# A two-layer graph network: the second pair of tiles prepared by the scheme of the later pairs

## The chip, the cores and the metric

The kernel runs on one core of a Trainium2 chip. The metric is the device time of one execution in microseconds (us); the time of a kernel is the median of its runs. Next to it stands one execution taken by the hardware profiler; all traces shown here are of such executions.

## What is computed

128 graphs of 64 nodes with 768 features (8192 rows) and one 0/1 adjacency matrix per graph go through two layers. Cut to what matters:

```python
# layer 0:  h = relu(layernorm(x));  deg, rdeg = row sums of adj and of its transpose, 0 replaced by 1
ctx = adj @ (h @ Wadj.T + badj) / deg  +  adj.T @ (h @ Wrev.T + brev) / rdeg  +  h @ Wself.T + bself
rel = einsum('bij,bijr->bir', adj, E[rels]) @ Wr.T + br * deg  +  (the same, turned: E[rr], Wrr, brr)
x = x + ctx + rel                      # rels is the adjacency matrix itself
# layer 1:  h = relu(layernorm(x))
#   attention over each graph's neighbours, six heads of 128; elu, and a sigmoid gate of h @ H_w.T
x = x + gate * elu(attention) + (1 - gate) * h
```

## The kernel before, in words

The 8192 rows are 64 tiles of 128 rows (two graphs each), taken in 32 pairs. Pass 1 computes layer 0 for one pair after the other, pass 2 layer 1. The change is in pass 1 alone.

For each pair the layer 0 product has a left operand of two rows of blocks (the two tiles) by three blocks of features, times three by three blocks of weights. Each block `a00` to `a12` of the left operand has three parts side by side: h gathered over the neighbours and divided by the row degree, the same for the turned adjacency, and the tile's own h. From the second pair on the 18 block products are done as 15, by a scheme in which sums of operand blocks (`f1`, `f7`, ..., formed on VectorE by `form`) meet sums of weight blocks (`g1`, ..., formed once by `weights_sums`). The relation part is a product of counts (how often each value stands in a row of the adjacency matrix, 81 columns) with a small table `tabs` of 16-bit numbers.

`main(p)` (line 792) gives the product steps of a pair: one matmul of 128x256 a step, six to a block product. Pair 0 has 108 of them, 18 for each fill of a PSUM bank, and two last count products; the other pairs have 90 and one. A bank of pair 0 takes a count product just before VectorE's `add` reads it (from the third fill on), so steps 53, 71, 89 and 107 are followed by one. The banks are `pwa`, `pwb` and the two halves of `pwcd`.

The order of the work is written out by hand, for every engine and for the queue of SyncE (SP), which issues nearly all transfers. `merged` (line 259) runs a pair's steps and calls each entry of a list just before the product step whose number it bears. For pair 0 that list is `first` (line 969), which prepares pair 1; for pair p it is `beside(p)` (line 1011), with the numbers of `BESIDE` (line 86), which prepares pair p+1 and finishes pair p-1. Each engine works its part of the program in this order; an instruction that waits holds all behind it on its engine.

A pair in `SHARED` (line 778) is prepared in another way than the others. Before the change that is every pair from 2 on. The two ways differ in these steps:

- Statistics for the norm: `dev` (line 931) calls `moments` on ScalarE for a pair in `SHARED`, and `deviation` (line 313) on VectorE for the others; the power is on GpSimd in both (lines 332 to 334, or line 321).
- Own part: the others multiply h by an identity along with the neighbours (`operands`, line 738, with n = 3 parts, so 192 columns, line 754). A pair in `SHARED` has n = 2 (128 columns). Its own part is written a second time by ScalarE in a mixed order (`relu_mixed`, line 549), turned in 32x32 blocks by VectorE (`turn_own`, line 558, one buffer `hpt` for all tiles), stored to DRAM (`put_own`, line 563) and loaded back into the third part of the six blocks (`load_own`, line 574) in runs of 32 floats.
- Operand sets: the others make them two blocks at a time (`operand`, line 775) in a PSUM tile `pb`. A pair in `SHARED` makes all six in one batch (`operands_in_one`, line 769); its last two blocks use the bank pair `pwcd`. ScalarE copies the sets out (line 764).
- Degrees: the others by a matmul with a block of ones (`degrees`, line 649) and a reciprocal on VectorE. A pair in `SHARED` reduces on VectorE, inverts, turns (`turn_degrees`, line 600), and spreads them through DRAM (`put_degrees`, `get_degrees`); `over_row_degrees` (line 622) makes the scaled adjacency.
- Counts: `spread_counts` (line 703) lays them out in `c3s`; the others turn them on TensorE (`count_t`, line 728) and copy them on ScalarE. A pair in `SHARED` turns them in blocks on VectorE (`turn_counts`) and goes through DRAM (`put_counts`, `get_counts`).

The table `tabs` is made of three parts in `table_part` (line 526): ScalarE rounds a part to 16 bits, VectorE takes the rest for the next, and SP stores it in its places (line 538). The count products of pair 0 are the first to read it.

Of the kernel before, what the change touches and what calls it, by code (L numbers as in the profile page):

```python
# [156 lines left out]
def kernel(  # L157
# [45 lines left out]
    nc = tc.nc  # L203
# [10 lines left out]
    NP = NT // 2  # L214
# [188 lines left out]
    with ExitStack() as px:  # L403
# [154 lines left out]
        def turn_own(t):  # L558

            h = HPT[t] = work.tile([P, D], F32, name="hpt", bufs=1)  # L560
            nc.vector.transpose(h, HP[t])

        def put_own(t):
            nc.sync.dma_start(H0D[t].rearrange("(b p) n -> p b n", p=P),
                              HPT[t].rearrange("p (b n) -> p b n", b=KB))
# [8 lines left out]
        def load_own(p, *names):  # L574

            for n in names:
                k, q = int(n[1]), int(n[2])
                nc.sync.dma_start(
                    new_operand(p, n)[:, 2].rearrange("p b (a n) -> p (b a) n", a=NQ),
                    H0D[2 * p + k].rearrange("(b i) (f n) -> (i f) b n", i=Q, n=Q)[  # L580
                        :, q * KQ * NQ : (q + 1) * KQ * NQ, :])
# [18 lines left out]
        def turn_degrees(p):  # L600


            row_degrees(p)
            d = dgs
            v = d[:, :4].rearrange("p (k d) -> p k d", k=2)
            nc.vector.tensor_scalar(v, DGR[p], 1.0, None, op0=OP.max)
            nc.vector.reciprocal(v, v)
            RD[p] = small.tile([P, Q], F32, name="dt", bufs=1)
            nc.vector.transpose(RD[p], d)

        def put_degrees(p):
            nc.sync.dma_start(RDD[p].rearrange("c (b n) -> b c n", n=Q), RD[p])

        def get_degrees(p):
            rd = RD[p] = work.tile([P, 4, N], F32, name="rd", bufs=1)
            for g in range(GT):
                at = RDD[p][0:4, g * N : (g + 1) * N]
                nc.sync.dma_start(rd[g * N : (g + 1) * N],
                                  bass.AP(tensor=at.tensor, offset=at.offset,
                                          ap=[[0, N], *at.ap]))  # L620

        def over_row_degrees(p):
            rd = RD[p].rearrange("p (k d) n -> p k d n", k=2)
            for d in range(2):
                nc.vector.tensor_mul(rts[p % 2][:, :, d, :], ADF[p][:, :, 1 - d, :], rd[:, :, d, :])

        def prep_c(p):


            af, ab = ADF[p], AB[p]  # L630
            cnt = CNT[p] = work.tile([P, 2, NROW], BF16, name="cnt", bufs=1)
            if p not in SHARED:
                row_degrees(p)
            dg = DGR[p]
            nc.vector.tensor_scalar(cnt[:, :, NCNT : NCNT + 2], dg, 1.0, None, op0=OP.min)
            nc.vector.memset(cnt[:, :, NCNT + 2 : NCNT + 3], 1.0)
            gr = GR[p] = work.tile([P, 2, 2, N], BF16, name="gr")
            wo = WO[p] = work.tile([P, 2, 2, N], BF16, name="wo")
            ov = work.tile([P, 2, 2, N], BF16, name="ov", bufs=1)
            nc.vector.tensor_scalar(ov, ab, float(NG), None, op0=OP.is_gt)  # L640
            nc.vector.tensor_scalar(wo, ov, float(DIGIT - 1), 1.0, op0=OP.mult, op1=OP.add)
            nc.vector.scalar_tensor_tensor(gr, ov, -float(NG), ab, op0=OP.mult, op1=OP.add)
            nc.vector.tensor_scalar(ov, ab, float(2 * NG), None, op0=OP.is_gt)
            nc.vector.scalar_tensor_tensor(wo, ov, float(DIGIT * DIGIT - DIGIT), wo,
                                           op0=OP.mult, op1=OP.add)
            nc.vector.scalar_tensor_tensor(gr, ov, -float(NG), gr, op0=OP.mult, op1=OP.add)
            SUM[p] = work.tile([P, 2, 2, NG], F32, name="sum")
# [38 lines left out]
        def count(p, k):  # L686
            ids_worth(p, k)
            ids_sum(p, k)
# [14 lines left out]
        def spread_counts(p):  # L703
            for f, n, at, v0, w in ((0, 3, 0, 0, Q), (3, 1, 0, Q, Q), (4, 2, 0, Q, Q), (6, 2, 0, 2 * Q, R2),
                                    (6, 1, R2, 2 * Q, Q - R2), (7, 1, R2, 3 * Q - R2, 2 * R2 - Q)):
                c3 = c3s.rearrange("p k i (f n) -> p k i f n" if p in SHARED else
                                   "p k i (n f) -> p k i f n", f=NQ)
                put = nc.gpsimd.tensor_copy if p in SHARED else nc.scalar.copy
                put(c3[:, :, f // NQ, f % NQ : f % NQ + n, at : at + w],
                    CNT[p][:, :, None, v0 : v0 + w].to_broadcast([P, 2, n, w]))  # L710

        def turn_counts(p):
            ct = CT_T[p] = work.tile([P, 4, P], BF16, name="ct", tag="eq", bufs=1)
            nc.vector.transpose(ct.rearrange("p a n -> p (a n)"),
                                c3s.rearrange("p k i n -> p (k i n)"))

        def put_counts(p):
            nc.sync.dma_start(CTD[p].rearrange("(q p) n -> p q n", p=P), CT_T[p])

        def get_counts(p):  # L720
            ct = work.tile([P, 2, 2, P], BF16, name="cntT", bufs=2)
            nc.sync.dma_start(
                ct.rearrange("p k i n -> p (k i n)").rearrange("p (b n) -> p b n", n=Q),
                CTD[p].rearrange("(b i) (f n) -> (i f) b n", i=Q, n=Q))
            for k in range(2):
                CT_T[p, k] = ct[:, k]

        def count_t(p, k):
            pn = pss.tile([P, 2, 512], F32, name="pb")[:, 0, :P].bitcast(BF16).rearrange(
                "p (i n) -> p i n", i=2)  # L730
            if k == 0:
                CT_T[p] = work.tile([P, 2, 2, P], BF16, name="cntT", bufs=2)
            cn = CT_T[p, k] = CT_T[p][:, k]
            for i in range(2):
                nc.tensor.transpose(pn[:, i, :], c3s[:, k, i, :], identb)
            nc.scalar.copy(cn, pn)

        def operands(p, *calls, last=False):


            n = 2 if p in SHARED else 3
            if last:
# [32 lines left out]
        def operand(p, *calls):  # L775
            operands_out(p, operands(p, *calls), *calls)

        SHARED = range(2, NP)

        def form(p, *names):  # L780

            for n in names:
                s0, x, s1, y = A_SUMS[n]
                if n in IN_PLACE:
                    OPS[p, n] = OPS[p, IN_PLACE[n]]
                else:
                    new_operand(p, n)
                signed(OPS[p, n], s0, OPS[p, x], s1, OPS[p, y])
# [155 lines left out]
        def norm(p, k):  # L944
            t = 2 * p + k
            if p not in SHARED:
                scaled_mean(*DEV[t])
            for f in (relu_mixed, relu) if p in SHARED else (relu,):
                f(t, DEV[t][0])
# [8 lines left out]
        def degrees_and_norms(p):  # L958
            deg(p)
            for k in range(2):  # L960
                norm(p, k)
            one_over(DEG[p])
            over_degrees(p, DEG[p])

        def weights_sums(*names):
            for n in names:
                sum_of_weights(bw, n)
# [14 lines left out]
            (23, lambda: prep(1)),  # L982
            (24, lambda: devs(1)),
            (26, lambda: table_part(2)),
            (34, lambda: degrees_and_norms(1)),
            (30, lambda: weights_sums("w", "v")),
            (36, lambda: weights_sums("g6")),
            (38, lambda: weights_sums("u", "g14")),
            (38, lambda: count_t(0, 0)),
            (40, lambda: prep_c(1)),  # L990
            (44, lambda: count(1, 0)),
            (45, lambda: count_t(0, 1)),
            (52, lambda: count(1, 1)),
            (54, lambda: operand(1, (1, 2))),
            (54, lambda: operand(1, (1, 1))),
            (58, lambda: digits(1)),
            (60, lambda: load(2)),
            (60, lambda: weights_sums("g12", "g5")),
            (64, lambda: operand(1, (0, 0))),
            (64, lambda: operand(1, (0, 2))),  # L1000
            (66, lambda: weights_sums("g8")),
            (73, lambda: form(1, "f1", "f7", "f4")),
            (76, lambda: weights_sums("g11", "g3")),
            (80, lambda: operand(1, (1, 0))),
            (80, lambda: operand(1, (0, 1))),
            (84, lambda: spread_counts(1)),
            (84, lambda: count_t(1, 0)),
            (91, lambda: form(1, "f8", "f9", "f2")),
            (92, lambda: count_t(1, 1))]

        def beside(p):

# [572 lines left out]
```

## Time and profile before

| | before |
|---|---|
| runs | 2323.54 to 2324.08 us |
| median of 3 runs | 2323.63 us |
| the profiled execution's own time | 2323.5 us |
| span of its trace (first to last instruction) | 2321.7 us |
| mean granted TensorE clock | 0.997 |

An engine's row in a timeline has the start in us from the span's start, the length, the engine, the line of the code and the instruction with what it writes and reads; "xN" are N instructions in a row, merged. In square brackets stands how long the engine was idle before, and what ended that. PE is TensorE's matmuls, PEld its weight loads, DVE is VectorE, ACT ScalarE, POOL GpSimd, and SPq the issue of transfers by SyncE. A product step of 32-bit numbers is two MATMUL records.

### The profile page before, as it was taken

How to read it: one execution, taken by the hardware profiler on the slowest of the kernel's cores; microseconds unless marked ns; L12 is line 12 of the kernel's file. 1: busy time of each engine (PE TensorE's matmuls, PEld its weight loads, DVE VectorE, ACT ScalarE, POOL GpSimd, SP SyncE). 2: the span in 40 equal slices, each digit the busy share in tenths (PEclk: the TensorE clock that was granted, in tenths of full speed). 3: DMA queues.
4: the chain of work that ended last, by engine and by line, in shares of the span. 5: the costliest groups of instructions: out<-in, count | busy, mean ns of one | idle time of the engine just before them, and what ended most of it. 6: DMA issues, size and time to landing. Idle time of an engine off the chain costs nothing.

```text
span 2321.7 us, 35387 instructions
## 1 busy us (share of the span) xinstructions
PE 2295.5 (99%) x11321; PEld 1638.6 (71%) x11321; DVE 1935.2 (83%) x3741; ACT 1319.2 (57%) x4083; POOL 309.4 (13%) x739
## 2 busy tenths in 40 slices
PE   9999999999999999999999999999999999999996
PEld 7888888888888888888888885444444444444444
DVE  8877777777777777777777777899999999999998
ACT  3454454454454444543543523777777777777776
POOL 1111111111111111111111111000001100000011
PEclk9999999999999999999999999999999999999998
DMA  5445545545546546546546555567666677667766
GB/s 191 92 100 130 136 101 135 130 101 136 129 101 146 118 103 147 116 108 148 110 107 151 109 140 165 138 159 166 157 163 159 158 173 168 158 157 168 168 158 144
DMA packets 831048, 321.68 MB, mean 139 GB/s; under 512 B 633236, under 2 KB 781063, under 8 KB 830860
## 3 DMA queue, kind: packets, MB, share of 16 engines
q1 hardware_dynamic: 821788, 294.99, 52.9%
q0 software_dynamic: 8928, 24.38, 5.9%
q8 instruction: 89, 1.46, 0.3%
q14 instruction: 99, 0.81, 0.1%
q10 hardware_dynamic: 144, 0.04, 0.0%
HBM read 151.90 MB, written 141.85 MB: 127 GB/s over the span
## 4 chain that ended last, share of the span: by engine, by line
PE 96%; DVE 2%; DMA 1%; issue 0%; SPq 0%; ACT 0%; DVEq 0%; ACTq 0%
PE pwa L826 21%; PE pwb L826 18%; PE pwcd L826 15%; PE pma L1143 14%; PE pmb L1143 12%; PE pmd L1143 5%; PE pmc L1143 5%; PE pb L754 3%; PE ps L1343 1%; PE pwcd L810 1%; PE pwcd L754 1%; DMA weights<-in_wadj_t_dram 1%; DVE f L1380 0%; PE pmc L1343 0%; PE pwa L810 0%
## 5 line engine op out<-in xcount | busy, mean ns | idle before, releaser
L826 PE MATMUL pwa<-weights,op 128*128 128x256 f32 x2304 | 529.6, 379 | 0.3 <-DVE x L818 0.3
L826 PEld LDWEIGHTS pwa<-weights,op 128*128 128x128 f32 x2304 | 427.5, 190 | 56.0 <-issue 1.1
L826 PE MATMUL pwb<-weights,op 128*128 128x256 f32 x1932 | 451.4, 381 | 0.0
L826 PEld LDWEIGHTS pwb<-weights,op 128*128 128x128 f32 x1932 | 361.9, 190 | 51.4 <-issue 0.8
L355 DVE TENSOR_TENSOR op<-op 128x768 f32<-128x768 f32 x310 | 290.2, 945 | 94.6 <-ACT op L764 91.7
L826 PE MATMUL pwcd<-weights,op 128*128 128x256 f32 x1560 | 357.8, 379 | 0.0
L826 PEld LDWEIGHTS pwcd<-weights,op 128*128 128x128 f32 x1560 | 296.1, 190 | 40.1
L1143 PE MATMUL pma<-weights,op_f 128*128 128x512 f32 x620 | 297.0, 593 | 0.1
L1196 ACT ACTIVATE pr<-pr 128x128 f32<-128x128 f32 x768 | 226.2, 297 | 68.5 <-DVE pr L1185 68.4
L764 ACT COPY op<-pb 128x512 f32<-128x512 f32 (+1 forms) x132 | 70.8, 618 | 331.9 <-PE pb L754 331.8
L1143 PEld LDWEIGHTS pma<-weights,op_f 128*128 128x128 f32 x620 | 117.5, 190 | 147.7 <-issue 125.4
L1143 PE MATMUL pmb<-weights,op_f 128*128 128x512 f32 x372 | 175.1, 592 | 0.0
L553 ACT ACTIVATE hp<-x,rn 128x768 f32<-128x768 f32 x60 | 109.3, 1821 | 108.3 <-POOL rn L334 108.3
L1196 ACT ACTIVATION_READ_ACCUMULATOR pr<-pr 128x1 f32 x768 | 145.0, 189 | 0.0
L326 ACT ACTIVATE hf<-x 128x768 f32<-128x768 f32 x64 | 53.6, 838 | 160.3 <-DVE x L862 148.7
L332 POOL TENSOR_SCALAR rn<-su 128x1 f32<-128x1 f32 x124 | 25.8, 208 | 844.8 <-ACT hf L327 527.9
L1143 PEld LDWEIGHTS pmb<-weights,op_f 128*128 128x128 f32 x372 | 70.7, 190 | 89.0 <-issue 87.3
L1143 PE MATMUL pmc<-weights,op_f 128*128 128x512 f32 x248 | 121.6, 592 | 0.0
L1303 ACT ACTIVATE pb<-a,mx 128x64 f32<-128x64 f32 x360 | 119.6, 335 | 2.2 <-DVE mx L1294 2.1
L818 DVE TENSOR_TENSOR x<-pwcd,x 128x256 f32<-128x256 f32 x127 | 53.3, 420 | 80.2 <-PE pwcd L810 80.0
L684 DVE TENSOR_REDUCE sum<-eq 128x26 f32<-128x1664 bf16 x64 | 120.0, 1876 | 0.1
L1143 PE MATMUL pmb<-weights,h 128*128 128x512 f32 x248 | 119.8, 604 | 0.0
(248 smaller groups left out, 3904.4 us busy)
## 6 DMA issues: line engine op xcount, KB each, us to landing
x<-in_x_dram SPq DMA_DIRECT2D x64, 384.0 KB
h<-ht SPq DMA_DIRECT2D x256, 96.0 KB
out_dram<-x SPq DMA_DIRECT2D x64, 384.0 KB
hh<-hh SPq DMA_DIRECT2D x64, 384.0 KB
h<-h SPq DMA_DIRECT2D x64, 384.0 KB
x<-hh SPq DMA_DIRECT2D x64, 384.0 KB
out_dram<-f POOLq DMA_DIRECT2D x62, 384.0 KB, 7.6
h<-hpt SPq DMA_DIRECT2D x60, 384.0 KB
```

The costliest lines, as they stand in the source:

```text
L326: nc.scalar.activation(by, src, AF.Copy, scale=-1.0 / D, accum_out=sums[:, 0:1])
L332: nc.gpsimd.tensor_scalar(to[:, 0:1], sums[:, 1:2], 1.0 / D, EPS, op0=OP.mult, op1=OP.add)
L355: return (nc.vector.tensor_add if s1 == "+" else nc.vector.tensor_sub)(to, x, y)
L553: nc.scalar.activation(hp.rearrange("p (b f i) -> p b f i", b=KB, f=NQ), X[t].rearrange("p (b i f) -> p b f i", b=KB, f=NQ), AF.Relu, scal ...
L684: nc.vector.tensor_reduce(SUM[p][:, k], EQ[p, k], AX.X, OP.add)
L754: nc.tensor.matmul(to[:, g, :, i, :], H0[2 * p + k][o, kb * P : (kb + 1) * P], rts[p % 2][o, k, :n].rearrange("p s n -> p (s n)"), start=T ...
L764: nc.scalar.copy(a[:, :n].rearrange("p s h (g n) -> p g (s h) n", g=GT), ps[:, :, c * n * KQ * N : (c + 1) * n * KQ * N].rearrange("p g (x ...
L818: nc.vector.tensor_add(v, bank[b][:, :CQ], v)
L826: nc.tensor.matmul(bank[b][:, :CQ], OPS[p, an][:, s, q, :], bw[bn][:, (s * KQ + q) * CQ : (s * KQ + q + 1) * CQ], start=(first and q == s ...
L1143: nc.tensor.matmul(bank[p, b], operand(p, an)[:, q, :], bw2[bn][:, 2 * q * CQ : 2 * (q + 1) * CQ], start=(first and q == 0), stop=(q == KQ ...
L1196: nc.scalar.activation(PR[t][:, j, h, :], PR[t][:, j, h, :], AF.Copy, accum_out=to)
L1303: nc.scalar.activation(PB[t][:, h, :], AL[t][:, h, :], AF.Exp, bias=MX[t][:, h : h + 1], accum_out=DN[t][:, h : h + 1])
```

## The change

Pair 1 joins the pairs in `SHARED`. The list `first` is rewritten for that. `degrees_and_norms(1)`, three `operand` calls and two `count_t` calls of pair 1 leave it. In their place come `turn_degrees`, `put_degrees`, `get_degrees`, two norms, two turns of the own part with their stores, `over_row_degrees`, `load_own` for all six blocks, the counts' turn with its store and load, and one `operands_in_one`. `count_t(0, 1)` moves from step 45 to 39, `spread_counts(1)` from 84 to 66, and `g11` and `g3` get places of their own. `load(2)` keeps its number 60 and stands behind `load_own` in SP's queue. Of the forms only `f1` and `f7` are left in the list; `f4`, `f8`, `f9` and `f2` are made in `beside(1)`, since line 1016 asks for `SHARED`. `dev(1, k)` uses `moments` for the same reason. In `spread_counts` pair 1 still uses ScalarE, with the layout of `SHARED`.

```diff
-                put = nc.gpsimd.tensor_copy if p in SHARED else nc.scalar.copy
+                put = nc.gpsimd.tensor_copy if p > 1 else nc.scalar.copy
...
-        SHARED = range(2, NP)
+        SHARED = range(1, NP)
...
             (23, lambda: prep(1)),
             (24, lambda: devs(1)),
             (26, lambda: table_part(2)),
-            (34, lambda: degrees_and_norms(1)),
+            (27, lambda: turn_degrees(1)),
+            (28, lambda: put_degrees(1)),
             (30, lambda: weights_sums("w", "v")),
             (36, lambda: weights_sums("g6")),
+            (38, lambda: get_degrees(1)),
             (38, lambda: weights_sums("u", "g14")),
             (38, lambda: count_t(0, 0)),
+            (39, lambda: count_t(0, 1)),
+            (40, lambda: norm(1, 0)),
+            (40, lambda: norm(1, 1)),
             (40, lambda: prep_c(1)),
+            (43, lambda: turn_own(2)),
+            (44, lambda: put_own(2)),
             (44, lambda: count(1, 0)),
-            (45, lambda: count_t(0, 1)),
+            (47, lambda: turn_own(3)),
+            (48, lambda: put_own(3)),
+            (50, lambda: over_row_degrees(1)),
             (52, lambda: count(1, 1)),
-            (54, lambda: operand(1, (1, 2))),
-            (54, lambda: operand(1, (1, 1))),
+            (54, lambda: load_own(1, "a01", "a00", "a02", "a10", "a11", "a12")),
             (58, lambda: digits(1)),
             (60, lambda: load(2)),
             (60, lambda: weights_sums("g12", "g5")),
-            (64, lambda: operand(1, (0, 0))),
-            (64, lambda: operand(1, (0, 2))),
+            (66, lambda: spread_counts(1)),
             (66, lambda: weights_sums("g8")),
-            (73, lambda: form(1, "f1", "f7", "f4")),
-            (76, lambda: weights_sums("g11", "g3")),
-            (80, lambda: operand(1, (1, 0))),
-            (80, lambda: operand(1, (0, 1))),
-            (84, lambda: spread_counts(1)),
-            (84, lambda: count_t(1, 0)),
-            (91, lambda: form(1, "f8", "f9", "f2")),
-            (92, lambda: count_t(1, 1))]
+            (70, lambda: turn_counts(1)),
+            (71, lambda: put_counts(1)),
+            (74, lambda: weights_sums("g11")),
+            (78, lambda: get_counts(1)),
+            (82, lambda: operands_in_one(1)),
+            (86, lambda: form(1, "f1", "f7")),
+            (90, lambda: weights_sums("g3"))]
```

## The prediction

> **What bounds the kernel now.** I read the page's busy shares first, then the chain that ended last, then the timelines of each engine over the first 120 us, because the change lives there. On the page:
>
> ```profile
> PE 2295.5 (99%) x11321; PEld 1638.6 (71%) x11321; DVE 1935.2 (83%) x3741; ACT 1319.2 (57%) x4083; POOL 309.4 (13%) x739
> PE 96%; DVE 2%; DMA 1%; issue 0%; SPq 0%; ACT 0%; DVEq 0%; ACTq 0%
> ```
>
> TensorE is busy for 99% and is 96% of the chain: whatever leaves TensorE's program in pass 1 shortens the run one for one, unless a wait replaces it. A query for TensorE's waits between 110 and 1300 us has no entry at all. The stretch concerned is the rest of pair 0. In the TensorE timeline (start, length, instructions; a "x32" row holds 16 product steps, each step being two records):
>
> ```profile
> 25.36 7.07 PE L826 MATMUL pwb<-weights,op 128*128 128x256 f32 x32
> 32.73 0.27 PE L654 MATMUL pb<-ab,blkb 128*128 128x256 bf16 x1 [0.29 <-ACT ab L589]
> 32.84 1.03 PE L826 MATMUL pwb<-weights,op 128*128 128x256 f32 x4
> 34.56 0.28 PE L735 MATMUL pb<-identb,c 128*128 128x128 bf16 x2
> 34.67 3.24 PE L826 MATMUL pwcd<-weights,op 128*128 128x256 f32 x14
> 41.80 0.38 PE L810 MATMUL pwcd<-tabs,cntT 128*128 128x256 bf16 x2
> 42.12 1.57 PE L754 MATMUL pb<-r,h 64*128 64x192 f32 x16
> 43.62 4.58 PE L826 MATMUL pwa<-weights,op 128*128 128x256 f32 x20
> 60.68 0.23 PE L735 MATMUL pb<-identb,c 128*128 128x128 bf16 x1 [0.17 <-ACT c L709]
> 72.66 2.75 PE L826 MATMUL pwb<-weights,op 128*128 128x256 f32 x12
> 115.91 2.76 PE L826 MATMUL pwb<-weights,op 128*128 128x256 f32 x12
> 152.50 2.06 PE L754 MATMUL pb<-r,h 64*128 64x128 f32 x32
> 154.38 1.06 PE L754 MATMUL pwcd<-r,h 64*128 64x128 f32 x16
> 159.16 2.75 PE L826 MATMUL pwb<-weights,op 128*128 128x256 f32 x12
> ```
>
> Pair 1 starts at 72.66, pair 2 at 115.91, pair 3 at 159.16: both take 43.25 us. At 42.12 one of the three n=3 operand sets (192 columns) of pair 1; at 152.50 the whole n=2 batch of a later pair. The only waits are 0.29, 0.17 and, at 72.15, another 0.29 for VectorE's read of a bank.
>
> The other engines in the same stretch (VectorE, ScalarE, GpSimd, the DMA queue):
>
> ```profile
> 30.55 0.24 DVE L699 CAST cnt<-di 128x156 bf16<-128x156 int32 x1
> 55.46 0.41 DVE L818 TENSOR_TENSOR x<-pwcd,x 128x256 f32<-128x256 f32 x1
> 32.58 0.83 ACT L532 CAST tl<-tv 81x768 bf16<-81x768 f32 x1
> 33.58 2.11 POOL L321 TENSOR_TENSOR rn<-ve,mhalf 128x1 f32<-128x1 f32 x1 [0.81 <-DVE ve L320]
> 34.17 2.73 SPq L538 DMA_DIRECT2D tabs<-tl  x4
> 82.29 0.61 SPq L612 DMA_DIRECT2D rd<-dt  x1
> 84.31 1.37 SPq L618 DMA_DIRECT2D rd<-rd  x2
> ```
>
> VectorE reads the pwcd bank at 55.46 although TensorE filled it at 42: its queue runs 13 us behind and without gaps. That queue is what a changed order can turn into a TensorE wait.
>
> **What the Trainium skill says.** "DMA: Bandwidth & Descriptors", section Anatomy of one DMA: a fixed cost of about 2.0 us per transfer. The trace agrees: L612 is issued at 82.29 and the load that waits for it at 84.31. Same page, Specifications: below 512 B per piece the line rate is not reached. Agrees: the weights came in at 348 GB/s (28 to 30 us), while 96 to 98 us, with only transfers in runs of 32 floats, shows 163 GB/s at a full DMA share. "SBUF — State Buffer", Who interferes with whom: a VectorE instruction with two SBUF inputs blocks a GpSimd instruction that reads SBUF. Agrees: the power on GpSimd took 2.11 at 33.58 beside L355 weight sums of 1.75 each, against 0.55 at 68.39. "TensorE: Matmul & The Clock Gate", Part 3: matmuls on different row groups overlap; the 64-row operand matmuls of 272 ns follow each other every 94 or 59 ns.
>
> **Taken from TensorE.** By place in the stream: from 25.36 (step 18 of pair 0) to 72.66 is 47.30 us. It holds 90 product steps at 2.59/6 = 0.432 us, 38.85; six count products at 0.22, 1.32; the wait of 0.29. What is left, 6.84, is all that was put in between: degrees(1), eight transposes, three operand sets, with the cost of each interruption. Pair 2 likewise: 43.25 - 38.85 - 1.32 = 3.08 for one n=2 batch with its interruption. Two of the transposes cost 0.11 (34.56 to 34.67) plus 0.06 by which the next seven steps exceed 7 x 0.432, so pair 0's own four stay as 0.34. New total 3.42; **saving 6.84 - 3.42 = 3.42 us**. Check by instruction: 48 x (94 - 59) ns = 1.7, degrees 0.57 (25.36 + 16 x 0.432 to 32.84), pair 1's transposes 0.46 + 0.11: 2.8; the other 0.6 is three interruptions become one. I keep 3.42, with 2.8 as its low end.
>
> **ScalarE and the table.** The moments of pair 1's two tiles move from VectorE to ScalarE ahead of the tl cast: 65.67 to 67.67, so 2.0 each, 4.0. The cast starts at 36.6 instead of 32.58 and ends at 37.4; its four DMAs take SP 2.73 (to 40.2) and land about 1.1 after the last issue (in the trace packets follow 0.6 to 1.1 after an issue ends): 41.3. TensorE reaches the first count product at 41.80 - 0.57 - small edges = 41.1. **A wait of about 0.3**; from 0 to 1.2 (landing a full 2.0 after the issue). The 0.29 wait for ab goes with degrees(1). The cntT copies now come before the norms and end at 38.1: no wait. The four norm activations (1.83 and 1.01, twice) end at 43.7; were each of GpSimd's six steps to take 2.11, the second norm would end at 50, still ahead of the operands at 54.
>
> **VectorE's queue in the new order.** It loses bn_stats and what follows (2.83), the mean scalings, clamp, reciprocal of 1.74 and products (3.2 in all), and later the forms f4, f8, f9, f2 (3.8, moved to pair 1). It gains two turns (0.90 each), turn_degrees (1.00), over_row_degrees (0.9), turn_counts (0.7). Walking it with the rows' durations: turn_degrees waits for af (32.4), ends 33.4; w, v 36.8; add 37.2; g6, u, g14 42.3; prep_c without its reduce 44.3; first turn 45.2; count 49.2; second turn 50.1; row degrees 51.0; count 54.9; **the pwcd add 55.3**; digits 56.0. Waits on the way: the first turn's input is ready at 39.9; the second turn shares one hpt buffer and needs the first put landed, 45.2 + 2.9 = 48.1, 1.1 ahead; the degrees return, put 40.2 behind the tl DMAs, back by 45.3, 4.8 ahead. Behind each of these on VectorE stands the pwcd add, and TensorE waits for that.
>
> **TensorE against it.** Step 82 with the batch falls at 41.34 + 0.3 + 28 x 0.432 + 0.22 = 54.0; its third set writes pwcd 1.9 later, 55.9: 0.5 after the add. ScalarE spreads the counts 56.0 to 57.4 and copies the three sets in 2.9 (110.45 to 113.32), to 60.3; TensorE opens pwcd anew at step 90, 54.0 + 3.1 + 8 x 0.432 + 0.22 = 60.7: 0.4 after. Both covers are thin: a microsecond more on VectorE costs up to 0.5. I take **0.1** here, 0 to 2 for the range.
>
> **Queues.** SP gets 13 more issues, 0.61 + 1.37 + 2 x 0.38 + 6 x 0.54 + 0.38 + 0.5, about 7 us, and load(2) moves behind load_own: from 37 to about 55. Own parts: six times 128 KB at 163 GB/s, 4.8; issued 50.5 to 54.6, landed by 58, while f1 reads them at 63.9 behind g11. Pair 2's first input is read after 60. The counts return by 67, first used at step 17 of pair 1, 77. All hidden; if the cover went, TensorE would stand at pair 1's first product (69.7).
>
> **Pair 1.** Four forms more beside g9 and g1: VectorE does f8, f4, f5, add, f9, g9 by 6.2 after the pair's start, the add of f1's bank by 6.6; that bank is written again at step 18, 7.8. Then it falls behind by up to 3 and is level by step 53, filling the 1.17 gap at 96.61. No wait expected, 0 to 1.
>
> **Sum** on the profiled execution (2323.5, span 2321.7 and 1.8 around it): -3.42 + 0.3 + 0.1 = -3.0, so 2320.5. Its time is 0.1 below the median of 2323.63, which gives **2320.6**.
>
> **Rivals.** (a) *Forecast*, small waits: 2320.6, chance 0.68. (b) *VectorE 2 to 4 us late*, so that both thin covers tear: TensorE waits some 2 in place of 0.4: 2322.2 and up to the time before; 0.18. For it: 22 us without a gap; against it: each input is ready over 1 us ahead. (c) *Slower*: the DRAM trips hold VectorE at the second turn or the row degrees, with the pwcd add behind. Slack 0.5 plus gain 3.0: it decides from 3.5 us lateness, that is a put that takes 7.5 us instead of 2.9. At 7 us of lateness 2323.6 + 7 - 3.5 = 2327.1; beyond 0.2% (4.6 us) from 8. Against it: the DMA share after 42 us was 0. Chance 0.10, of which 0.07 beyond 0.2%. (d) *No wait at all* and the 0.29 gone too: 2319.9; 0.04. That the edit might do nothing is excluded: the operand width follows from SHARED.
>
> **Chances and range.** About 0.2% is what a measurement of this kernel can tell from no change. Beyond it on the fast side I see 0.02, slow 0.07, within 0.91. The range 2319.8 to 2323.2 covers (a), (d) and most of (b).
>
> **What would show it.** Right: 64x128 operands of pair 1 in one batch near 54 to 57, no L654 and only four L735 in pass 1 after the start, pair 1 beginning near 69.7 and lasting 43.25. A wait of 0 to 1 on tabs at 41. Wrong: TensorE waiting on DVE x L818 near 56 or on ACT op L764 near 60 by more than 1; pair 1 longer than 43.5; L561's second turn starting after 51.

## The result and the profile after

The changed kernel takes 2320.24 us (median of 22 runs, 2319.55 to 2321.51), the kernel before 2323.53 (22 runs, 2321.89 to 2324.44): 3.3 us less, a ratio of 0.9987 with a 95% interval of 0.9981 to 0.9993. The two ranges do not overlap. The forecast was 2320.6. The profiled execution took 2319.8, its span is 2318.0. The page's lines on the busy shares and on the chain, for the changed kernel:

```profile
PE 2294.2 (99%) x11316; PEld 1638.0 (71%) x11316; DVE 1933.6 (83%) x3735; ACT 1324.0 (57%) x4091; POOL 320.1 (14%) x743
PE 96%; DVE 2%; DMA 1%; issue 0%; SPq 0%; POOL 0%; ACT 0%; DVEq 0%; POOLq 0%; ACTq 0%
```

Nothing has changed hands: TensorE is still the bound and only its program is shorter. Where, its timeline shows (start, length, instructions):

```profile
25.45 7.93 PE L826 MATMUL pwb<-weights,op 128*128 128x256 f32 x36
34.08 0.28 PE L735 MATMUL pb<-identb,c 128*128 128x128 bf16 x2
34.68 0.28 PE L735 MATMUL pb<-identb,c 128*128 128x128 bf16 x2
41.32 0.38 PE L810 MATMUL pwcd<-tabs,cntT 128*128 128x256 bf16 x2
53.95 2.06 PE L754 MATMUL pb<-r,h 64*128 64x128 f32 x32
55.83 1.06 PE L754 MATMUL pwcd<-r,h 64*128 64x128 f32 x16
68.59 0.38 PE L810 MATMUL pwa<-tabs,cntT 128*128 128x256 bf16 x2
69.27 0.38 PE L810 MATMUL pwcd<-tabs,cntT 128*128 128x256 bf16 x2 [0.30 <-DVE x L818]
69.49 2.75 PE L826 MATMUL pwb<-weights,op 128*128 128x256 f32 x12
112.73 2.75 PE L826 MATMUL pwb<-weights,op 128*128 128x256 f32 x12
```

The degrees matmul and four of the transposes are gone, and the operands stand in one batch at 53.95. The only wait left in the stretch is the 0.30 that was there before. I measure all that follows by one stretch, from the first product of the pwb fill (25.45) to the first product of pair 1 (69.49): **44.04 us, against 47.30 before**. Pair 1 takes 43.24 (69.49 to 112.73), pair 2's start moves by 3.18, and the attention batches seen near 1705 and 2197 are 3.18 and 3.01 earlier. Only the very end differs by more: the spans by 3.7. The runs of one kernel spread over 2 us. TensorE's own program repeats far better: pair 1 takes 43.24 or 43.25 in every trace of this document, and a difference of 0.1 in the stretch counts. So the stretch carries the verdicts, from one trace for each kernel, and the medians are set beside it.

The other engines around it, VectorE, ScalarE, GpSimd and SP's queue, with the rows that correspond to those of before:

```profile
32.49 0.42 DVE L598 TENSOR_REDUCE dg<-af 128x4 f32<-128x256 f32 x1 [1.61 <-ACT af L588]
54.26 0.41 DVE L818 TENSOR_TENSOR x<-pwcd,x 128x256 f32<-128x256 f32 x1
36.45 0.82 ACT L532 CAST tl<-tv 81x768 bf16<-81x768 f32 x1
40.86 2.07 POOL L333 TENSOR_TENSOR rn<-rn,mhalf 128x1 f32<-128x1 f32 x1
37.30 2.75 SPq L538 DMA_DIRECT2D tabs<-tl  x4
40.15 0.59 SPq L612 DMA_DIRECT2D rd<-dt  x1
50.55 4.69 SPq L578 DMA_DIRECT2D op<-h  x6
```

VectorE waits 1.61 for af (the adjacency matrices as 32-bit numbers) and is then without a gap up to the pwcd read, which ends at 54.67: 1.16 ahead of the third operand set at 55.83. That 1.16 is the cover of this read. The table's last part leaves SP at 40.05 and the count product starts at 41.32 without a wait.

### The profile page after: what moved, and what is told of

Read it like the earlier page. It is cut to its first block, busy times and chain, and to the rows that moved or that the text cites. A ratio compares the mean times of both kernels' runs of the same rounds, so it can differ in the third digit from the quotient of the medians.

```text
span 2318.0 us, 35403 instructions
## 1 busy us (share of the span) xinstructions
PE 2294.2 (99%) x11316; PEld 1638.0 (71%) x11316; DVE 1933.6 (83%) x3735; ACT 1324.0 (57%) x4091; POOL 320.1 (14%) x743
## 4 chain that ended last, share of the span: by engine, by line
PE 96%; DVE 2%; DMA 1%; issue 0%; SPq 0%; POOL 0%; ACT 0%; DVEq 0%; POOLq 0%; ACTq 0%
PE pwa L826 21%; PE pwb L826 18%; PE pwcd L826 14%; PE pma L1149 14%; PE pmb L1149 12%; PE pmd L1149 5%; PE pmc L1149 5%; PE pb L754 3%; PE ps L1349 1%; PE pwcd L754 1%; PE pwcd L810 1%; PE pmc L1349 0%; DVE f L1386 0%; DMA out_dram<-f 0%; PE pwa L810 0%
## 5 line engine op out<-in xcount | busy, mean ns | idle before, releaser
L826 PEld LDWEIGHTS pwcd<-weights,op 128*128 128x128 f32 x1560 | 296.2, 190 | 40.2
L332 POOL TENSOR_SCALAR rn<-su 128x1 f32<-128x1 f32 x126 | 30.6, 243 | 847.0 <-ACT hf L327 525.5
```

The costliest lines, as they stand in the source:

```text
L332: nc.gpsimd.tensor_scalar(to[:, 0:1], sums[:, 1:2], 1.0 / D, EPS, op0=OP.mult, op1=OP.add)
L826: nc.tensor.matmul(bank[b][:, :CQ], OPS[p, an][:, s, q, :], bw[bn][:, (s * KQ + q) * CQ : (s * KQ + q + 1) * CQ], start=(first and q == s ...
```

## The experiments

Every kernel is the changed one with an edit (e11_degrees45, e10_rest_counts and e12_table_first with a second one), so a stretch above 44.04 is what the edit costs. The kernel before was measured again beside each group of runs. Its median there is in the fourth column, and the ratio is to that one.

| kernel | stretch | median, us | before, beside it | ratio to before, 95% |
|---|---|---|---|---|
| before | 47.30 | 2323.53 | | |
| changed | 44.04 | 2320.24 | 2323.53 | 0.9987 (0.9981 to 0.9993) |
| e1_degrees | 46.82 | 2322.74 | 2323.53 | 0.9997 (0.9988 to 1.0006) |
| e11_degrees45 | 45.54 | 2320.94 | 2322.91 | 0.9991 (0.9985 to 0.9998) |
| e2_counts | 44.37 | 2320.40 | 2323.53 | 0.9987 (0.9980 to 0.9994) |
| e3_sets | 44.83 | 2321.01 | 2323.53 | 0.9989 (0.9980 to 0.9997) |
| e4_own | 46.05 | 2322.77 | 2323.53 | 0.9998 (0.9989 to 1.0006) |
| e9_stats | 44.19 | 2320.30 | 2323.66 | 0.9986 (0.9980 to 0.9993) |
| e5_late2 | 45.18 | 2321.40 | 2323.66 | 0.9991 (0.9985 to 0.9998) |
| e6_late4 | 48.95 | 2325.57 | 2323.66 | 1.0008 (1.0000 to 1.0017) |
| e7_table | 45.54 | 2321.56 | 2323.66 | 0.9992 (0.9984 to 1.0001) |
| e8_rest | 43.58 | 2319.28 | 2323.09 | 0.9984 (0.9977 to 0.9990) |
| e10_rest_counts | 43.86 | 2319.70 | 2323.09 | 0.9986 (0.9979 to 0.9992) |
| e12_table_first | 43.28 | 2319.09 | 2322.91 | 0.9984 (0.9977 to 0.9990) |

### One part undone at a time

**The own part.**

```diff
-            n = 2 if p in SHARED else 3
+            n = 2 if p > 1 else 3
...
-            (82, lambda: operands_in_one(1)),
+            (79, lambda: operand(1, (1, 2))), (79, lambda: operand(1, (1, 1))),
+            (83, lambda: operand(1, (0, 0))), (83, lambda: operand(1, (0, 2))),
+            (87, lambda: operand(1, (1, 0))), (87, lambda: operand(1, (0, 1))),
```

The turns, their stores and `load_own` go, and `f1`, `f7` move to 88.

> The changed kernel with the own part of pair 1 multiplied by the identity again (three parts, 192 columns; no turn, store or reload), six sets in three places. Theory (program length): 48 x 35 ns = 1.7 and two more interruptions, 0.3: a stretch of about 46.0, some 2322.2 in all. Rival (the own part's trip brings a wait that hides part of the gain): clearly less than 1.7 more.

Measured 46.05, so 2.01 more, as the theory said: 1.7 for the wider products and 0.3 for two more interruptions. The six `operand` calls stand at three steps, as in the list before. The own part by the identity, with these interruptions, is the largest share of the saving, and its trip through DRAM costs no wait that would eat it.

**The counts.** `turn_counts`, `put_counts` and `get_counts` of pair 1 go, `count_t(1, 0)` comes before step 86 and `count_t(1, 1)` before 92, with the layout that they need.

> The changed kernel with the counts of pair 1 turned on TensorE again, in two places (before steps 86 and 92). Theory (program length): four transposes and two interruptions come back, plus 0.34 to 0.57, a stretch of 44.4 to 44.6. Rival (covers are thin, so anything inserted late in pair 0 lets VectorE or ScalarE catch up and costs nothing): 44.0 to 44.1.

Measured 44.37, 0.33 more. The program's length counts here too, and neither place has slack that would take the work in for nothing.

**The degrees.**

```diff
-            (27, lambda: turn_degrees(1)),
-            (28, lambda: put_degrees(1)),
...
-            (38, lambda: get_degrees(1)),
...
-            (50, lambda: over_row_degrees(1)),
+            (34, lambda: degrees_again(1)),   # ones matmul, reduce, reciprocal, products
```

> The changed kernel with the degrees of pair 1 made by the ones matmul again. The measure is the stretch from the first pwb product of pair 0 to the first product of pair 1, 44.04 us in the changed kernel and 47.30 before. Theory (TensorE's program length alone counts, all covers hold): plus 0.57, 44.6, about 2320.8 in all. Rival (the trip of the degrees through DRAM is itself on the path): the stretch gets shorter than 44.04.

This missed: 46.82, 2.78 more. TensorE's timeline in e1_degrees shows why:

```profile
32.78 0.27 PE L654 MATMUL pb<-ab,blkb 128*128 128x256 bf16 x1 [0.29 <-ACT ab L589]
37.44 0.27 PE L735 MATMUL pb<-identb,c 128*128 128x128 bf16 x2 [2.06 <-DVE rd L656]
```

The matmul's result sits in one of two PSUM tiles until VectorE reads it at 36.97, behind the sums w and v (v itself stood 2.57 for a transfer, by the trace); with the second transposes moved from step 45 to 39, they now ask for that tile too early. The move of `count_t(0, 1)` suits the new scheme only. So I put it back:

> As e1_degrees, the degrees of pair 1 by the ones matmul, but with the second pair of pair 0's transposes back at step 45. In e1_degrees TensorE stood 2.06 at step 39 for a PSUM tile that VectorE had not yet read (line 656, behind the sums w and v). Theory (that wait came from the place of the transposes, and the price of the degrees proper is 0.57): no such wait, a stretch of 44.6. Rival (keeping the ones matmul costs the whole 2.8 that e1_degrees showed): 46.8, with the wait at another place.

45.54. The wait of 2.06 is gone, and the stream up to the first count product is 0.57 longer than in the changed kernel (25.37 to 41.81 against 25.45 to 41.32), the price that was reckoned, with a wait of 0.30 for ab (the same matrices as 16-bit numbers) in it. The remaining 0.9 is another wait:

```profile
57.12 1.16 PE L754 MATMUL pwcd<-r,h 64*128 64x128 f32 x16 [0.63 <-DVE x L818]
35.25 1.76 DVE L355 TENSOR_TENSOR weights<-weights 128x1536 f32<-128x1536 f32 x1 [2.60 <-DMA tabs<-tq]
```

VectorE's reciprocal and products for the matmul's way make its pwcd read end at 57.07 in place of 54.67, and the cover of 1.16 is torn. Where they stand matters: they come behind the sum v, for which VectorE has stood idle 2.60 (second line), while `turn_degrees` in the changed kernel is done by 33.6, ahead of both sums. Neither theory nor rival had that: the degrees' turn through DRAM saves 0.57 on TensorE and keeps VectorE on time as well.

**One batch or three sets.**

```diff
-            (82, lambda: operands_in_one(1)),
+            (82, lambda: operand(1, (1, 2), (1, 1))),
+            (84, lambda: operand(1, (0, 0), (0, 2))),
+            (86, lambda: operands_out(1, operands(1, (1, 0), (0, 1), last=True), (1, 0), (0, 1))),
```

> The changed kernel with the same three operand sets of two parts before steps 82, 84 and 86 in place of one batch. No instruction more. Theory (an interruption of the product stream has a price of its own, 0.1 to 0.2 each): 44.2 to 44.45. Rival (only the number and width of the matmuls count): 44.04; then the part of the saving that the sum by instruction left open has another source.

44.83: the same instructions cost 0.79 more, 0.4 for each further interruption, twice what I expected. In e3_sets:

```profile
53.87 1.16 PE L754 MATMUL pb<-r,h 64*128 64x128 f32 x16
54.96 1.13 PE L826 MATMUL pwb<-weights,op 128*128 128x256 f32 x4
56.02 1.16 PE L754 MATMUL pb<-r,h 64*128 64x128 f32 x16
```

A set lasts 1.09 to the next product, against 1.88/2 = 0.94 inside the batch, and the two steps behind it 1.06 in place of 2 x 0.432 = 0.86. No wait is shown for either, and why the set itself takes longer stays open. For the sets of the kernel before, with 192 columns, the price is smaller: a set lasts 1.50 to the next product (42.12 to 43.62), which is 16 times 94 ns, so that only some 0.2 around it is left. e4_own's 0.3 for two interruptions agrees. Interruptions are thus about half of the 0.6 that the prediction's check by instruction left over. Where the rest lies is said further down, with the steps of the prediction.

**The statistics.** `dev(1, k)` uses `deviation` again, and the norms `scaled_mean`.

> The changed kernel with the norm statistics of pair 1 on VectorE again (bn_stats, 2.83 us, and two scalings). Theory (VectorE idles 1.61 for af in the changed kernel, which takes up part of it): the pwcd add is 1.3 later, 0.14 beyond its cover: stretch 44.1 to 44.3. Rival (the move of the statistics to ScalarE keeps VectorE on time and so carries the gain): a wait of 1.7, stretch 45.7.

44.19. The pwcd read starts at 55.23 instead of 54.26 and ends at 55.64, still inside the cover, by 0.11. So the number came as forecast, but not by the forecast wait: 0.06 lies at the batch (2.93 to the next product against 2.87) and 0.10 in the pwcd fill behind it (7.87 against 7.77), with no wait shown. Moving 2.83 us of work to ScalarE was worth 0.15: VectorE had waited 1.61 for af anyway.

### How thick the covers are

**VectorE late by 2 and by 4 us.** The two comparisons of `count(1, 1)` are done once and twice more ahead of the pwcd read:

```diff
-            (52, lambda: count(1, 1)),
+            (52, lambda: (ids_worth(1, 1), count(1, 1))),                      # e5_late2
+            (52, lambda: (ids_worth(1, 1), ids_worth(1, 1), count(1, 1))),     # e6_late4
```

> The changed kernel with 2.05 us of VectorE work done twice (the two comparisons of count(1, 1)) ahead of the pwcd add of pair 0. In the changed kernel's trace that add ends at 54.67 and the third operand set starts at 55.83, a cover of 1.16. Theory (the cover is the whole story): TensorE waits 2.05 - 1.16 = 0.9 at the third set and nothing more at step 90, where ScalarE's copies are as late as TensorE is: stretch 44.9. Rival (lateness runs on to the second cover and to f1 as well): 46.0 and more.

45.18, 1.14 more: an idle time of 0.84 on TensorE, and 0.28 beside it that shows as no wait (the batch to the next product is 3.99 against 2.87). No second wait follows.

> As the last, with 4.1 us more VectorE work ahead of the pwcd add. Theory: a wait of 2.95, stretch 47.0, the whole gain of the change gone: 2323.2. Rival (f1 and f7 or the copies become a second wait): 48 and more, slower than the kernel before.

48.95, and 2325.57 in all: slower than before. The wait is the expected one, and no second engine wait follows it, so the rival's number came without its reason. But the eight product steps behind it take 5.24 where e5_late2 has 3.55:

```profile
59.43 1.16 PE L754 MATMUL pwcd<-r,h 64*128 64x128 f32 x16 [2.96 <-DVE x L818]
60.52 5.41 PE L826 MATMUL pwb<-weights,op 128*128 128x256 f32 x16
65.76 0.38 PE L810 MATMUL pwb<-tabs,cntT 128*128 128x256 bf16 x2
```

The table by stretches of e6_late4 (busy us and count on PE, PEld, DVE, ACT, POOL, then the granted TensorE clock, DMA share, GB/s) shows the reason:

```profile
60.00:61.00 1.00, 1.00 (x14) 0.85 (x11) 1.00 (x2) 0.80 (x5) 0.00 (x0) 0.98 0.91 359
61.00:62.00 1.00, 1.00 (x5) 0.74 (x4) 1.00 (x2) 1.00 (x5) 0.00 (x0) 0.50 0.18 71
64.00:65.00 1.00, 1.00 (x5) 0.83 (x5) 1.00 (x1) 1.00 (x4) 0.00 (x0) 0.82 0.00 0
```

TensorE was granted half its clock for 3.4 us (60.96 to 64.37), which costs 1.7 more. The slow time begins 1.5 us after TensorE has resumed. Without it the stretch would be about 47.3, level with the kernel before; the median is 1.9 above before's, so it is not the traced execution's alone.

The Trainium skill, "TensorE: Matmul & The Clock Gate", Part 1, describes such a gate: half the clock after an idle window of about 3.4 us, until a busy one has passed, with a window that runs freely. The length of the slow stretch agrees; that the gap need be 3.4 us long does not, here 2.96 did it. Nor does the length of the wait alone decide. Near the end of pass 2 there is a wait of 3.17 or 3.18 in all traces but e9_stats. In eleven of them the clock is at half beside it, for 3.4 us or twice that. In e5_late2 and e11_degrees45 it stays full, and in e9_stats it falls to half at 2272.95, one us after a wait of 1.84:

```profile
2277.85 1.10 PE L1452 MATMUL pmc<-weights,op_f 128*128 128x256 f32 x4 [3.17 <-DVE f L1386]
2278.00:2279.00 1.00, 1.00 (x5) 0.88 (x6) 1.00 (x1) 1.00 (x3) 0.00 (x0) 1.00 0.92 129
2271.98 0.29 PE L1350 MATMUL ps<-hx,pT 64*64 64x128 f32 x1 [1.84 <-DMA pT<-pt]
2273.00:2274.00 1.00, 1.00 (x17) 0.67 (x10) 0.05 (x1) 0.00 (x0) 0.00 (x0) 0.50 0.00 0
```

The first two lines are of e5_late2, the others of e9_stats. A window that runs freely would fit this; no run here tests it. The waits of 2.06 (e1_degrees) and 0.84 (e5_late2) in pair 0 left the clock at full.

**The table late.** `table_part(2)` moves from 26 to 40, ahead of the norms.

> The changed kernel with the last table part rounded after ScalarE's two count copies, 0.65 later. Packets of the table's last transfer end at 40.75 in the changed kernel and the first count product starts at 41.3, so the cover is 0.3 at most. Theory (predicted tabs wait is real but was just missed): TensorE waits 0.35 to 0.6, stretch 44.4 to 44.6. Rival (the transfer lands much earlier than reckoned): no wait, 44.04.

45.54: a wait of 1.33 for the table, 1.50 by place, that is from the start of the count product to the next product (41.24 to 42.96, less the 0.22 of a count product). So the cover is thin, but my size was wrong. ScalarE's cast is only 0.43 later. In SP's queue, though, the degrees' put and get had come ahead of the table:

```profile
34.88 0.62 SPq L612 DMA_DIRECT2D rd<-dt  x1
37.50 1.34 SPq L618 DMA_DIRECT2D rd<-rd  x2
38.94 2.85 SPq L538 DMA_DIRECT2D tabs<-tl  x4
```

The get waits on SP until the put has landed, and holds the table behind it. In the changed kernel the degrees stand behind the table.

### A shorter stretch still

**The last count products.** Pair 0's two last count products both go to bank pwa in the course of the third pwcd fill:

```diff
-            rest_of = ["12"] if p else ["00", "10"]
...
+                for i, c in ((93, "00"), (104, "10")):
+                    steps[i] = lambda f=steps[i], c=c: (f(), counts("a", c, True), add("a", c))
...
-            (90, lambda: weights_sums("g3"))]
+            (95, lambda: weights_sums("g3"))]
```

> The changed kernel with the two last count products of pair 0 both in bank pwa, in the course of the third fill (after the products of steps 93 and 104) instead of at the end, and g3 at 95. Theory: the wait of 0.30 for VectorE's read of pwcd ahead of pair 1 goes, minus perhaps 0.1 for two interruptions: stretch 43.75 to 43.85, 2320.0. Rival (the wait moves to bank pwa or to pair 1's first product): 44.0 or more.

43.58, 0.46 less; 2319.28 us. That is the whole price of the wait, which shows 0.30 of idle time: in the changed kernel the count product ahead of it takes 0.68 (68.59 to 69.27) where others take 0.22. The two places inside the fill cost nothing beyond their own 0.22.

**The counts of pair 0 through DRAM too.** `count_t(0, k)` go; `turn_counts(0)` and `put_counts(0)` come at 24, `get_counts(0)` at 25, ahead of the last table part.

> As the last, and the counts of pair 0 turned on VectorE and taken through DRAM too (between the first and the last table part in SP's queue). Theory: four transposes fewer, minus 0.34: stretch 43.4 to 43.5, 2319.6; VectorE is 0.3 later than in the changed kernel, within its cover of 1.16. Rival (the load of the counts holds SP, so the table lands late): a wait on tabs of 0.3 to 1.5 near 41, stretch 43.8 to 45.

43.86, the rival: the get sat on SP until 37.27 for its put and sent the table off at 37.72, for a wait of 0.45, 0.61 by place (41.40 to 42.23). So the table part was put ahead of the get, and its rounding ahead of ScalarE's statistics:

> As e10_rest_counts, with the last table part rounded ahead of ScalarE's statistics of pair 1 and sent ahead of the load of pair 0's counts. Theory: the wait of 0.45 on the table goes, and the saving of 0.34 over e8_rest shows: a stretch of 43.2 to 43.3, about 0.3 less than e8_rest. Rival (the counts now land after the first count product wants them): a wait near 41, stretch 43.6 or more.

43.28 and no wait; 2319.09 us. SP's queue in e12_table_first:

```profile
34.34 0.38 SPq L717 DMA_DIRECT2D ct<-ct  x1
35.03 2.76 SPq L538 DMA_DIRECT2D tabs<-tl  x4
37.89 0.38 SPq L721 DMA_DIRECT2D cntT<-ct  x1
```

It has the shortest stretch, 0.76 less than the changed kernel. By time neither it nor e8_rest is shown to be faster than the changed kernel: their ratios to before (0.9977 to 0.9990 for both) overlap its own. Only the traces tell the three apart.

## Why the prediction was right, step by step

- **Taken from TensorE**: predicted 3.42. The stretch lost 3.26, with no new wait. The parts by experiment are 2.01 for the own part with its interruptions, 0.57 for the degrees (with their wait of 0.29) and 0.33 for the counts, 2.91 in all. The other 0.35 is a wait at the counts in the kernel before: there two transposes take 0.46 (60.29 to 60.75), and 0.11 without a wait.

```profile
60.29 0.22 PE L735 MATMUL pb<-identb,c 128*128 128x128 bf16 x1
60.68 0.23 PE L735 MATMUL pb<-identb,c 128*128 128x128 bf16 x1 [0.17 <-ACT c L709]
60.75 2.81 PE L826 MATMUL pwb<-weights,op 128*128 128x256 f32 x12
```

- **Where the term was 0.16 too large**: the prediction set the last wait of pair 0 apart as 0.29. By place it costs 0.45 in the kernel before (71.77 to 72.44, less 0.22), and it stays. So 0.16 was counted among the work that goes. The 0.6 left over in the check by instruction, put down to interruptions alone, is this 0.16, 0.1 in the products behind pair 1's transposes and some 0.3 for two interruptions.
- **ScalarE and the table**: predicted a wait of 0.3, measured none, so this step was off. The landing of 1.1 was right: in e7_table and e10_rest_counts the product that waited starts 1.05 and 1.08 after the last transfer has left SP (41.79 to 42.84, 41.04 to 42.12). In the changed kernel SP is done at 40.05 in place of 40.2, and TensorE comes at 41.32 in place of 41.1, since the "small edges" were not there. e7_table shows that the threat was real.
- **VectorE's queue**: predicted a pwcd read ending at 55.3 and a cover of 0.5; measured 54.67 and 1.16. Most of the difference is `over_row_degrees`, 0.9 reckoned and about 0.4 taken (49.98 to 50.35). e5_late2 and e11_degrees45 show that this cover is the first to tear.
- **The two wrong sizes work against each other**: 3.42 - 0.4 against 3.26 - 0, so 3.0 was forecast where the stretch shows 3.26 and the medians 3.3. The mechanism, a shorter program on TensorE with covers that hold, is what the traces show; that the total came this close is in part luck.
- **Queues**: `load_own` left SP from 50.55 to 55.24, as reckoned (50.5 to 54.6), and the counts came back without a wait. From a store's issue to that of the load that waits for it the traces show no fixed time: 2.02 for the degrees before (82.29 to 84.31), 2.06 in the changed kernel, 2.62 in e7_table, and 2.96 for the counts in e10_rest_counts. GpSimd's norm steps took 4.3 a tile beside VectorE's weight sums of 1.75 each, against 1.7 at 67.84 before, for the most part beside shorter sums (0.95); the second norm ended at 46.1, still ahead of its turn at 49.09. (The 272 ns of the prediction is the length of a 128-column operand matmul; those of 192 columns last 323.)
- **Pair 1**: no wait and 43.24, as forecast.
- **The rivals**: what came lies between (a) and (d): none of the small waits, but the 0.30 ahead of pair 1 stayed. (b) did not come; e5_late2 gives its price, 1.1 for 2 us of lateness. (c) put the point from which lateness makes the kernel slower at 3.5. With the measured cover it would have been 1.16 + 3.26 = 4.4, and e6_late4 was slower at 4.1 already, because of the clock, which the rival did not have.

## What to carry to other kernels

Where one engine is busy for 99%, count the cost of what stands in its stream by position, from one product to the next of an undisturbed row, and not by instruction: interruptions, and the full price of a wait, show only there. In this kernel work moved to other engines and through DRAM was free as long as the read that frees a buffer stayed on time; find that read and its cover. On an issuing queue, put a load that waits for its own store behind whatever else is due, not ahead of it.

## What was not expected of the hardware

- One more interruption of a row of 128-row products by a set of 64-row ones cost 0.4 us without a wait in the trace for sets of 128 columns (e3_sets, 0.79 for two), and less than 0.2 for sets of 192 (e4_own, 0.3 for two).
- A wait of 2.96 on TensorE brought half the clock for 3.4 us, 1.7 on top of the wait. Its length does not settle it: a wait of 3.17 left the clock full in two traces, and one of 1.84 was followed by half the clock in another.
- A wait costs more than its idle time in the trace: 0.28 more ahead of the third operand set (0.84 idle, 1.12 longer), 0.16 to 0.17 more at count products (1.33 and 1.50 in e7_table, 0.45 and 0.61 in e10_rest_counts).
